# A second receiver for turned attention tiles in batch 3 of a convolution and attention kernel

## The chip, the cores and the metric

The kernel runs on one core of a Trainium2 chip. The metric is the device time of one execution in microseconds (us), the median of three runs. An execution is one launch of the whole program on one set of inputs; all data is float32.

## The reference, cut to what matters

The input is four images (batches) of 128 channels by 64 x 64 positions. Layer 0 normalises by groups, takes a deformable 3 x 3 convolution (bilinear samples at computed places, then a matrix product) and adds it to the input. Layer 1 treats each image as 4096 tokens of 128 channels. What the change touches is its attention:

```
qkv    = _qz_ring(heads + rx_theta)                 # 16 heads of 8 numbers a token
scores = einsum('bhsd,bhtd->bhst', q, q) / sqrt(8)  # q is both query and key
attn   = softmax(scores, axis=-1)
ctx    = einsum('bhst,bhtd->bhsd', attn, q)         # and value
t      = t + _ln(x1 + ffn_out, ...)                 # projection, feed-forward, norms
t      = t + experts(_ln_t(t))                      # top 2 of 8 experts
```

Since q is query and key, the scores are symmetric: the exponentials of the scores between the tokens s and t serve for the queries s and, transposed, for the queries t. There is no causal mask, so each batch has 16 heads x 4096 x 4096 exponentials if no use is made of this.

## The kernel before, in words

**Tiling.** The 4096 tokens of a batch are 8 chunks of 512, and the 16 heads are 4 groups of 4. A *run* is the attention of one group for the 512 queries of one chunk (batch b, group g, chunk sc). A *step* of a run takes 128 keys (t from 0 to 31, four to a chunk): `scores` (L1261) makes four matmuls into two PSUM tiles `sc`, ScalarE makes two exponentials `e<-sc` of 128 x 1024 (L1270), and `context` (L1281) multiplies the exponentials with values and a column of ones into `acc`, which holds both the weighted sum and the denominator. There are three `sc` tiles and six `e` tiles. At the end of a run VectorE copies `acc` to `cu` (L1493) and it is parked in DRAM.

**Giving and taking.** `gifts(b, g, sc)` (L1295) names the chunks to which a run gives: before, the next one. For each given key tile, `turn` (L1135 to L1156) transposes the two `e` tiles in blocks of 32 on VectorE (L1140) into a tile `st` (three buffers, `NST`), and SyncE (SP) stores it to a DRAM slot `etd` (L1149, 1 MB). `add_run` leaves the taken key tiles out of the taker's list `ts` and spreads the given ones evenly over the giver's. The taker fetches each tile with one transfer on SP's queue (`fetch`, L1189, the transfer at L1195, 1 MB) into a buffer `et` (`NET` = 2 buffers), and `from_turned` (L1201) multiplies it into `acc` in two halves of 8 matmuls (L1214): it replaces four score matmuls, two exponentials and four context matmuls of a step. `granted` and `returned` count the `et` buffers; a fetch that finds none waits in `asking`, and is issued when a tile has been multiplied.

**Order of the runs.** Batch 3 goes chunk by chunk, and in a chunk over its four groups (`LOTS[3]`). Its chunk 0 takes nothing and has 32 steps a run; chunks 1 to 7 take 4 tiles from the chunk before and have 28 steps a run. That is 912 steps in batch 3, of 3700 in all.

**The order on the engines is fixed when the program is built.** The main loop (from L1417) emits the steps for PE, VectorE, GpSimd and SP by hand; each engine executes its list in order. Between two steps the planner `Beside` (L65) adds pieces of side work: the next batch's preparation, the turned halves (job "turned", rank -1, so ahead of all else), and *finishes* (`finish`, L1084: projection, feed-forward and experts of one chunk, with about forty short groups of matmuls, each with VectorE work behind it). It keeps a model clock that advances by 1.82 a step, lets one piece with matmuls in per step, gains 0.44 of PE time a step at most (`RATE`), and puts a piece off while VectorE's planned work is too far behind. Up to two finishes are open at a time; a chunk is finished after its fourth group. What is still open after the last step is emitted by `beside.drain()`, one job after the other. At the end of each run `drain("turned")` emits what is left of the taken tiles.

**Other transfers.** Before each run its keys and values (`kT` 256 KB and `qf` 72 KB a chunk, L1239 and L1241) are loaded chunk by chunk, also on SP's queue, leaving out the chunks that are taken. The buffer `xs` (18 KB a partition, one buffer) holds the gathered samples for the convolution; its last use is batch 3's preparation, which is over before batch 3's runs begin.

Of the kernel before, what the change touches and what calls it, by code (L numbers as in the profile page):

```python
# [9 lines left out]
F32 = mybir.dt.float32  # L10
# [12 lines left out]
P = 128  # L23
# [5 lines left out]
CH = 512  # L29
NCH = NPOS // CH  # L30
KK = 9
# [17 lines left out]
NET = 2  # L49
# [153 lines left out]
def need(pe=0.0, dve=0.0, lat=0.0, hold=False, after=0.0):  # L203

    return pe, dve, lat, hold, after
# [17 lines left out]
def kernel(  # L225
# [23 lines left out]
    NB = x.shape[0]  # L249
# [4 lines left out]
    big = ctx.enter_context(tc.tile_pool(name="big", bufs=1))  # L254
    work = ctx.enter_context(tc.tile_pool(name="work", bufs=2))
# [5 lines left out]
    beside = Beside()  # L261
# [156 lines left out]
    for i in range(NFX):  # L418
        t = big.tile([P, 4, QR], F32, name=f"fx{i}")
        nc.gpsimd.memset(t, 0.0)  # L420
        h = t[:, :, : HEADS * QW].rearrange("p j (h d) -> p j h d", d=QW)
# [735 lines left out]
    def etd_slot(g, sc, t):  # L1157
        key = g, t // 4 % 3, t // 4 - sc, t % 4
        if key not in etd:
            etd[key] = dram.tile([P, 4, 4 * P], F32, name="etd" + "_".join(map(str, key)))  # L1160
        return etd[key]

    room = [NET]
    asking = []

    def granted(emit):
        if room[0]:
            room[0] -= 1
            emit()
        else:  # L1170
            asking.append(emit)

    def returned():
        if asking:
            asking.pop(0)()
        else:
            room[0] += 1

    def fetch_values(run):
        b, g, _ = runs[run][:3]  # L1180
# [5 lines left out]
            )  # L1186
            values[run, giver] = q

    def fetch(run, giver, kt):  # L1189
        _, g, sc = runs[run][:3]  # L1190
        t = 4 * sc + kt
        if (g, giver, t) in turning:
            beside.flush()
        e = work.tile([P, 4, 4, P], F32, tag="et", name=f"et{run}_{giver}_{kt}", bufs=NET)
        nc.sync.dma_start(  # L1195
            out=e.rearrange("p r h x -> p r (h x)"),
            in_=etd_slot(g, giver, t).rearrange("(r i) o x -> i o r x", i=32),
        )
        fetched[run, giver, kt] = e, beside.now + 16.0

    def from_turned(run, acc):  # L1201

        for giver in takes[run]:
            qv = values.pop((run, giver)).rearrange("p t x -> p (t x)")
            for kt in range(4):
                while (run, giver, kt) not in fetched:
                    yield need(lat=1.0)
                e, landed = fetched.pop((run, giver, kt))
                for half in range(2):
                    yield need(pe=MM256, hold=None, after=landed)  # L1210
                    for t in (2 * half, 2 * half + 1):
                        for h in range(4):
                            at = QG * t + QW * h
                            nc.tensor.matmul(  # L1214
                                acc[32 * h : 32 * h + QW, P * kt : P * (kt + 1)],
                                lhsT=qv[:, at : at + QW],
                                rhs=e[:, :, h, 32 * t : 32 * (t + 1)],
                                start=False, stop=False,
                            )
                returned()  # L1220

    keys, queries, values = {}, {}, {}
    turning, storing = set(), set()
# [2 lines left out]
    fetched = {}  # L1226
# [67 lines left out]

    def gifts(b, g, sc):  # L1295
        first = (4 if g == NGRP - 1 else 3) if b == 0 else 0
        return [sc + 1] if first <= sc < NCH - 1 else []


    def add_run(b, g, sc, chunks, kind):  # L1300
# [55 lines left out]
    for n, (run, t) in enumerate(steps):  # L1356
        b, g, sc = runs[run][:3]
# [32 lines left out]
    def at_hand(step, n):  # L1390

        run, t = steps[step]
        b, g, sc = runs[run][:3]
        wanted = [(b, g, t // 4)]

        def missing():
            return any(l[0] in wanted and l[3] <= step for l in loads)

        if missing():
            load_next(n, wanted)  # L1400
        load_queries(run)
        if missing() or run not in queries:
            return False
        early = b == 0 and run < opening + 40
        return not early or max([landing[run]] + [landing[k] for k in wanted]) <= beside.now

    es = []
    n = issued = begun = 0
    beside.rate = 1.0
    with tc.manual_schedule(engines={PE, DVE, SP, POOL}):  # L1410
        alone.append(True)
        beside.add("prepare", prepare(0), 2)
        while (0, 0) not in prepared:
            beside.force("prepare")
        beside.flush()
        alone.clear()
        while n < len(steps):  # L1417
            if issued < len(steps) and issued <= n + LAG and at_hand(issued, n):
                es.append(scores(*steps[issued]))
                issued += 1  # L1420
            elif issued <= n:
                if beside.has("prepare"):
                    beside.force("prepare")
                else:
                    beside.now += beside.STEP
                    beside.flush(beside.now)
                continue
            run, t = steps[n]
            b, g, sc, ts, kind = runs[run]
            following = runs[run + 1] if run + 1 < len(runs) else None  # L1430
            at = n - ends[run]
            streaming = run < opening
            for m in (n, n + 1):
                if m < issued and steps[m] in gives:
                    gives.remove(steps[m])
                    turn(es[m - n], *steps[m])

            beside.fills = 3 if run < 12 else 1
            if streaming:
                backlog = 1.5  # L1440
            else:
                backlog = 0.4 if at >= len(ts) - 3 else 3.2
            if b + 1 < NB:

                share = (n - begun) / (of_batch[b] - 80 - begun)
                beside.rank("prepare", 2 if progress.get(b + 1, 0.0) > share else 0.5)
            beside.step(backlog)
            if issued <= n + LAG and issued < len(steps) and at_hand(issued, n):
                continue
            load_next(n)  # L1450
            if t == ts[0]:
                if kind in (MORE, LAST):
                    if (g, sc) in storing:
                        beside.flush()
                    cu = work.tile([P, 512], F32, tag="cu", name=f"cu{run}", bufs=NCU)
                    nc.sync.dma_start(out=cu, in_=partd[g][sc])
                if run == opening:
                    beside.rate = beside.RATE
                acc = ps_a.tile([P, 512], F32, tag="acc", name=f"acc{run}")
                if not beside.has("prepare") and b + 1 < NB and (b + 1, 0) not in prepared:  # L1460
                    beside.rate = beside.RATE
                    begun = n
                    beside.add("prepare", prepare(b + 1), 2)
            if at == len(ts) - 1:
                beside.drain("turned")
            if following:
                if following[0] != b and at == 0:
                    beside.drain("prepare")

                if at == 1:  # L1470
                    load_queries(run + 1)
                    if len(ts) <= 8 and run + 2 < len(runs):
                        load_queries(run + 2)
                if takes[run + 1] and at == len(ts) - 5:
                    fetch_values(run + 1)
                    for giver in takes[run + 1]:
                        for kt in range(4):
                            granted(lambda a=(run + 1, giver, kt): fetch(*a))
            by_act = run < opening
            context(acc, run, t, es.pop(0), cu if by_act and kind == MORE else None)  # L1480
            n += 1
            if at == 0 and takes[run]:
                beside.add("turned", from_turned(run, acc), -1)
            if at < len(ts) - 1:
                continue
            if not by_act:
                beside.dve = max(beside.dve, beside.now + 1.9) + ve(512)
            if kind in (WHOLE, FIRST):
                cu = work.tile([P, 512], F32, tag="cu", name=f"cu{run}", bufs=NCU)
            if by_act:  # L1490
                nc.scalar.copy(cu, acc)  # L1491
            elif kind in (WHOLE, FIRST):
                nc.vector.tensor_copy(cu, acc)  # L1493
            else:
                nc.vector.tensor_tensor(cu, cu, acc, ALU.add)
            if kind in (WHOLE, LAST):
                park_context(b, g, sc, cu)
            else:
                park_sums(g, sc, cu, beside.now + 3.0 if by_act else beside.dve)
        alone.append(True)  # L1500
        beside.drain()
# [73 lines left out]
```

## Time and profile before

| what | value |
|---|---|
| runs | 7573.33, 7592.69, 7599.12 us; median 7592.69 |
| profiled execution | 7579.71 us; its span from first to last instruction 7576.5 us |
| mean granted TensorE clock | 0.968 |
| busy, share of the span | PE 94%, ScalarE (ACT) 91%, VectorE (DVE) 59%, GpSimd (POOL) 22% |
| exponentials `e<-sc` | 7400 of 1081 ns (they overlap: 6849.4 us in all) |
| turned tiles | 396 stored, 396 fetched, 1 MB each |
| all DMA | 1689.51 MB, mean 223 GB/s |
| last exponential ends | 7491.9 us after the start |

The page of a profile gives the busy time of each engine, the span in 40 slices, the chain of work that ended last and the costliest groups of instructions. A view by stretches gives the busy time of each engine between two times, the granted clock, and the share and rate of the 16 DMA engines; a timeline lists the instructions of an engine by start and duration. Matmul ends are modelled, so the distance between starts says more of PE than its busy share. Batch 3's runs lie between about 5805 and 7492 us.

### The profile page before, as it was taken

How to read it: one execution, taken by the hardware profiler on the slowest of the kernel's cores; microseconds unless marked ns; L12 is line 12 of the kernel's file. 1: busy time of each engine (PE TensorE's matmuls, PEld its weight loads, DVE VectorE, ACT ScalarE, POOL GpSimd, SP SyncE). 2: the span in 40 equal slices, each digit the busy share in tenths (PEclk: the TensorE clock that was granted, in tenths of full speed). 3: DMA queues.
4: the chain of work that ended last, by engine and by line, in shares of the span. 5: the costliest groups of instructions: out<-in, count | busy, mean ns of one | idle time of the engine just before them, and what ended most of it. 6: DMA issues, size and time to landing. Idle time of an engine off the chain costs nothing.

```text
span 7576.5 us, 180754 instructions
## 1 busy us (share of the span) xinstructions
PE 7113.9 (94%) x73848; PEld 2375.9 (31%) x73848; DVE 4465.9 (59%) x8950; ACT 6863.5 (91%) x7467; POOL 1653.2 (22%) x1326
## 2 busy tenths in 40 slices
PE   3688999899999999999999999999999999999997
PEld 2122222223333333333333323333333333333333
DVE  7755356667444877776544677775444554455434
ACT  0578999889999999999999998989999999999995
POOL 5544034443000433422000334431000000000000
PEclk6889999999999999999999999999999999999998
DMA  6777567978446878887655789897454466666661
GB/s 181 223 204 219 141 223 241 300 234 291 149 168 200 292 244 280 268 277 244 203 179 190 228 279 298 289 324 237 174 190 152 148 236 230 232 222 239 226 202 63
DMA packets 909788, 1689.51 MB, mean 223 GB/s; under 512 B 150754, under 2 KB 384124, under 8 KB 858268
## 3 DMA queue, kind: packets, MB, share of 16 engines
q1 hardware_dynamic: 809102, 1371.37, 54.9%
q0 software_dynamic: 92160, 302.06, 12.4%
q8 instruction: 579, 9.49, 0.5%
q10 hardware_dynamic: 7694, 4.52, 0.2%
q14 instruction: 253, 2.07, 0.1%
HBM read 1027.51 MB, written 650.14 MB: 221 GB/s over the span
## 4 chain that ended last, share of the span: by engine, by line
PE 80%; DMA 8%; DVE 4%; issue 2%; ACT 2%; SPq 1%; another core or an unknown queue 0%; POOL 0%; POOLq 0%; DVEq 0%; ACTq 0%
PE acc L1281 39%; PE sc L1261 24%; PE acc L1214 5%; PE e_ps L281 4%; PE conv_ps L281 3%; DMA et<-etd 2%; PE f_ps L281 2%; ACT e L1270 2%; DMA etd<-st 1%; DMA sT<-smd 1%; PE om_ps L533 1%; DMA smd<-tr 1%; DVE st L1140 1%; DVE v L645 1%; DMA cu<-part 1%
## 5 line engine op out<-in xcount | busy, mean ns | idle before, releaser
L1270 ACT ACTIVATE e<-sc 128x1024 f32<-128x1024 f32 x7400 | 6849.4, 1081 | 527.0 <-PE sc L1261 368.1
L1281 PE MATMUL acc<-e,qf 128*9 128x512 f32 (+1 forms) x29600 | 3938.3, 601 | 18.6 <-ACT cu L1491 7.5
L1261 PE MATMUL sc<-qT,kT 32*128 32x512 f32 x14800 | 2368.7, 499 | 153.3 <-ACT e L1270 84.8
L1261 PEld LDWEIGHTS sc<-qT,kT 32*128 32x128 f32 x14800 | 942.8, 183 | 3612.6 <-ACT e L1270 3130.4
L625 POOL DMA_INDIRECT v<-tab,idx x1152 | 1451.8, 1260 | 1579.3 <-DVE tr L686 956.2
L1140 DVE STREAM_TRANSPOSE st<-e 128x1024 f32<-128x1024 f32 x792 | 937.3, 1222 | 752.4 <-ACT e L1270 620.1
L1281 PEld LDWEIGHTS acc<-e,qf 128*9 128x9 f32 (+1 forms) x29600 | 682.4, 91 | 610.3 <-issue 346.8
L396 POOL TENSOR_TENSOR r<-ln_t,expo 128x4 f32<-128x4 f32 x96 | 112.2, 1169 | 3105.4 <-DVE ln_t L394 3057.0
L645 DVE TENSOR_TENSOR v<-v,wt 128x1536 f32<-128x1536 f32 x384 | 667.0, 1737 | 119.5 <-DMA v<-tab,idx 96.8
L1214 PE MATMUL acc<-et,qv 128*9 128x128 f32 x12672 | 506.4, 276 | 52.2 <-DMA et<-etd 44.6
L1065 DVE TENSOR_TENSOR eo<-e_ps,gt 128x512 f32<-128x512 f32 x256 | 175.2, 686 | 552.5 <-PE e_ps L281 547.5
L650 DVE TENSOR_TENSOR v<-v 128x768 f32<-128x768 f32 x384 | 367.2, 956 | 10.1
L281 PE MATMUL conv_ps<-sT,wconv_sb 128*32 128x256 f32 x4320 | 351.0, 399 | 15.7 <-DMA sT<-smd 11.6
L1214 PEld LDWEIGHTS acc<-et,qv 128*9 128x9 f32 x12672 | 270.0, 90 | 254.4 <-issue 212.6
L686 DVE STREAM_TRANSPOSE tr<-v 128x128 f32<-128x128 f32 x1080 | 249.4, 282 | 37.5 <-DMA etd<-st 28.7
L1493 DVE COPY cu<-acc 128x512 f32<-128x512 f32 x116 | 80.2, 692 | 306.3 <-PE acc L1281 260.8
L651 DVE TENSOR_TENSOR v<-v 128x384 f32<-128x384 f32 x384 | 215.7, 562 | 13.3
L396 POOL TENSOR_TENSOR rstd<-lt_t,expo 128x4 f32<-128x4 f32 x32 | 57.9, 1811 | 575.9 <-DVE lt_t L394 550.7
L281 PE MATMUL f_ps<-w_sb,h 128*32 128x128 f32 x4096 | 166.1, 282 | 0.1
L950 DVE TENSOR_SCALAR h<-h_ps,b_sb 128x512 f32<-128x512 f32 x128 | 94.9, 744 | 100.3 <-PE h_ps L948 89.9
L823 POOL COPY fx<-rn 128x512 f32<-128x512 f32 x32 | 26.8, 838 | 526.3 <-DVE rn L822 321.4
L965 DVE TENSOR_TENSOR a<-a,f_ps 128x512 f32<-128x512 f32 x32 | 21.9, 685 | 198.8 <-PE f_ps L281 198.8
(227 smaller groups left out, 3166.9 us busy)
## 6 DMA issues: line engine op xcount, KB each, us to landing
etd<-st SPq DMA_DIRECT2D x396, 1024.0 KB
et<-etd SPq DMA_DIRECT2D x396, 1024.0 KB
kT<-kTd SPq DMA_DIRECT2D x372, 256.0 KB
smd<-tr SPq DMA_DIRECT2D x360, 192.0 KB
sT<-smd SPq DMA_DIRECT2D x360, 192.0 KB
qT<-qTd SPq DMA_DIRECT2D x166, 256.0 KB
atd<-cu SPq DMA_DIRECT2D x128, 256.0 KB
qf<-fqd SPq DMA_DIRECT2D x372, 72.0 KB
```

Of the source, the lines that this page charges most:

```text
L281: nc.tensor.matmul(dst[c : c + 32], lhsT=lhsT[:, c : c + 32], rhs=rhs, start=start, stop=stop)
L625: nc.gpsimd.indirect_dma_start(out=v[:, k, :], out_offset=None, in_=tab, in_offset=bass.IndirectOffsetOnAxis(ap=idx[:, j, kk : kk + 1], ax ...
L645: nc.vector.tensor_tensor(v4, v4, w12[:, :, None].to_broadcast([P, 12, C]), ALU.mult)
L650: nc.vector.tensor_tensor(v[:, :, : 2 * C], v[:, :, : 2 * C], v[:, :, 2 * C :], ALU.add)
L651: nc.vector.tensor_tensor(v[:, :, :C], v[:, :, :C], v[:, :, C : 2 * C], ALU.add)
L686: nc.vector.transpose(out=tr9[:, k, :, j % 4, :], in_=v[:, k, :C].rearrange("p (c i) -> p c i", i=32),)
L1065: nc.vector.tensor_tensor(ws[hf], pe.rearrange("p (e c) -> p e c", c=C), gt[:, i, 4 * hf : 4 * (hf + 1), None].to_broadcast([P, 4, C]), AL ...
L1140: nc.vector.transpose(out=st[:, :, 2 * pr : 2 * pr + 2, :].rearrange("p o h (q j) -> p o (h q) j", j=32), in_=es[pr].rearrange("p h (q o i ...
L1214: nc.tensor.matmul(acc[32 * h : 32 * h + QW, P * kt : P * (kt + 1)], lhsT=qv[:, at : at + QW], rhs=e[:, :, h, 32 * t : 32 * (t + 1)], star ...
L1261: nc.tensor.matmul(ps[i // 2][:, i % 2, :], lhsT=kT[h : h + 32, P * (t % 4) : P * (t % 4 + 1)], rhs=qT[h : h + 32, :], start=True, stop=True,)
L1270: nc.scalar.activation(e, ps[pr], AF.Exp, scale=1.0 / math.sqrt(HD))
L1281: nc.tensor.matmul(acc[32 * h : 32 * h + width, :], lhsT=flat[:, first : first + width], rhs=es[h // 2][:, h % 2, :], start=(t == ts[0]), ...
```

## The change

In batch 3, chunks 0, 2 and 4 give to the next chunk and to the one after. So chunks 2, 4 and 6 take 8 tiles a run (24 steps, before 28), and chunks 0, 2 and 4 turn 8 (before 4). Two views into the `xs` buffer, each of the size of one turned tile, are added as places for received tiles six steps before the end of batch 2's last run; `room` becomes a list of places, and a fetch into one of them is planned to land after 10 instead of 16 of the model clock. Nothing else differs.

```diff
-    room = [NET]
+    room = [None] * NET
     asking = []
 
     def granted(emit):
-        if room[0]:
-            room[0] -= 1
-            emit()
+        if room:
+            emit(room.pop(0))
         else:
             asking.append(emit)
 
-    def returned():
+    def returned(place):
         if asking:
-            asking.pop(0)()
+            asking.pop(0)(place)
         else:
-            room[0] += 1
+            room.append(place)
...
-    def fetch(run, giver, kt):
+    def fetch(run, giver, kt, place):
...
-        e = work.tile([P, 4, 4, P], F32, tag="et", name=f"et{run}_{giver}_{kt}", bufs=NET)
+        e = place
+        if e is None:
+            e = work.tile([P, 4, 4, P], F32, tag="et", name=f"et{run}_{giver}_{kt}", bufs=NET)
...
-        fetched[run, giver, kt] = e, beside.now + 16.0
+        fetched[run, giver, kt] = e, place, beside.now + (16.0 if place is None else 10.0)
...
     def gifts(b, g, sc):
         first = (4 if g == NGRP - 1 else 3) if b == 0 else 0
-        return [sc + 1] if first <= sc < NCH - 1 else []
+        if not first <= sc < NCH - 1:
+            return []
+        return [sc + 1, sc + 2] if b == NB - 1 and sc in (0, 2, 4) else [sc + 1]
...
+                if following[0] == NB - 1 != b and at == len(ts) - 6:
+                    spare_et = big.tile([P, KK, CH], F32, tag="xs", name="spare_et")
+                    spare_et = spare_et.rearrange("p k n -> p (k n)")
+                    for i in range(2):
+                        place = spare_et[:, 4 * CH * i : 4 * CH * (i + 1)]
+                        room.append(place.rearrange("p (r h x) -> p r h x", r=4, h=4))
```

More of the change, by code (lines that the diff above doesn't have):

```diff
@@ L1207, in from_turned @@
                     yield need(lat=1.0)
-                e, landed = fetched.pop((run, giver, kt))
+                e, place, landed = fetched.pop((run, giver, kt))
                 for half in range(2):
@@ L1219, in from_turned @@
                             )
-                returned()
+                returned(place)
     keys, queries, values = {}, {}, {}
@@ L1477 @@
                         for kt in range(4):
-                            granted(lambda a=(run + 1, giver, kt): fetch(*a))
+                            granted(lambda place, a=(run + 1, giver, kt): fetch(*a, place))
             by_act = run < opening
```

## The prediction

> **What bounds the kernel now.** I read the page first, then batch 3 by stretches of one chunk, then the timelines of PE and of the end. The stretches give per chunk: length, busy time (and count) of PE, PEld, DVE, ACT, POOL, then granted clock, DMA share and GB/s. Here are chunks 0, 2, 4, 6 and 7.
>
> ```profile
> 5805.00:6041.00 236.00, 235.91 (x2309) 75.69 (x2305) 135.46 (x320) 235.98 (x259) 7.05 (x7) 1.00 0.44 144
> ...
> 6249.00:6456.00 207.00, 206.62 (x2340) 71.40 (x2338) 104.02 (x228) 206.52 (x227) 4.03 (x4) 1.00 0.67 231
> ...
> 6663.00:6870.00 207.00, 206.26 (x2346) 71.56 (x2342) 103.41 (x215) 206.74 (x228) 3.02 (x3) 1.00 0.65 223
> ...
> 7077.00:7284.00 207.00, 207.00 (x2335) 71.21 (x2327) 95.75 (x189) 206.94 (x227) 3.02 (x3) 1.00 0.67 229
> 7284.00:7492.00 208.00, 207.69 (x2378) 73.07 (x2382) 60.78 (x189) 207.74 (x228) 5.34 (x5) 1.00 0.41 132
> ```
>
> ScalarE never idles, DVE is half free, and the DMA engines stand at two thirds. PE's column is full too, so one step has to be looked at (start, duration, group, on PE):
>
> ```profile
> 6522.38 0.51 PE L1261 MATMUL sc<-qT,kT 32*128 32x512 f32 x4
> 6522.82 0.62 PE L1214 MATMUL acc<-et,qv 128*9 128x128 f32 x16
> 6523.26 1.04 PE L1281 MATMUL acc<-e,qf 128*9 128x512 f32 x8
> 6524.23 0.51 PE L1261 MATMUL sc<-qT,kT 32*128 32x512 f32 x4
> ```
>
> From start to start, scores take 0.44, a turned half 0.44, the context 0.97: 1.85 us a step, and 1.41 without the half. On ACT, 36 exponentials took 33.32 us, 0.925 each, so 1.85 a step as well. Steps without a half last about as long (scores at 6516.53, 6518.28, 6520.11), so ScalarE sets the pace of batch 3 and PE just keeps up. 912 steps by 1.85 make 1687 us, the length of the stretches.
>
> The second thing that counts is the end. The last exponential ends at 7491.9 and the span at 7576.5, so 84.6 us hold no attention at all, only finishes: half of the experts of chunk 6, then all of chunk 7. On VectorE (start, duration, group):
>
> ```profile
> 7503.93 0.69 DVE L892 COPY y_6T<-y_ps 128x512 f32<-128x512 f32 x1 [0.57 <-PE y_ps L890]
> 7504.54 0.54 DVE L1097 RECIPROCAL rd<-rd 128x64 f32<-128x64 f32 x1
> 7505.00 0.63 DVE L899 TENSOR_TENSOR r<-r,vec_sb 128x512 f32<-128x512 f32 x1
> 7510.16 0.69 DVE L901 TENSOR_TENSOR aT<-aT,a 128x512 f32<-128x512 f32 x1 [4.54 <-DMA a<-rdd]
> ...
> 7545.56 0.69 DVE L892 COPY u_7T<-u_ps 128x512 f32<-128x512 f32 x1 [0.57 <-PE u_ps L890]
> ...
> 7572.14 0.69 DVE L892 COPY y_7T<-y_ps 128x512 f32<-128x512 f32 x1 [0.57 <-PE y_ps L890]
> ```
>
> A finish that stands alone takes 68.2 us (7503.93 to 7572.14), its part from the copy of u on 26.6 (7545.56 to 7572.14). It is a chain of short dependent instructions: DVE is busy for 41.7 us of it.
>
> **The change part by part.**
>
> *Steps that go.* Three chunks x 4 groups x 4 tiles = 48 steps, 96 exponentials. At 1.85 that is **-88.8 us**, all on the bounding engine, if nothing else is late.
>
> *Turned halves on PE.* 48 x 0.88 = 42 us come, 48 x 1.41 = 68 us go, and a step with a half still fits 1.85: nothing.
>
> *Turning on DVE.* 96 transposes of 1.22 us, 117 us in chunks 0, 2 and 4. In a run of chunk 2 that is 8 x 2.44 = 19.5 us of 44.4, beside a DVE that was busy for half: nothing by itself. But each reads two of the six e tiles and writes one of three st tiles, so if a store is late, the turn waits, then the e tiles, then ScalarE.
>
> *Transfers.* 48 stores and 48 fetches of 1.05 MB come, 101 MB; some key loads go. A run of chunk 2 or 4 now moves 16 x 1.05 = 16.8 MB of tiles, 6 x 0.336 of keys and values, about 1.0 of the rest: 19.8 MB. The same count for a run before gives 11.3 in 51.8 us, 219 GB/s, beside rows of 223 to 231. In 24 x 1.85 = 44.4 us 19.8 MB need 446 GB/s. The trace shows no such rate. In stretches of 6 us where the DMA share is about 1 or over, I find 294 to 409 GB/s, mean 359 over 50 of 220 stretches of batch 3. Two of them:
>
> ```profile
> 6634.00:6640.00 6.00, 6.00 (x92) 2.30 (x84) 5.39 (x12) 6.00 (x8) 0.00 (x0) 1.00 1.07 377
> 7046.00:7052.00 6.00, 6.00 (x66) 1.94 (x58) 4.18 (x8) 6.00 (x8) 0.00 (x0) 1.00 1.04 409
> ```
>
> At 360 a run takes 55.0 us, 10.6 over its steps: 42 a chunk. Some of that can be put off into the next, lighter chunk: three stores (3.1 MB, 9 us) and about 5 us of the lead of the first four fetches. So 28 a chunk, 56 for chunks 2 and 4. Chunk 6 takes 8 and gives 4: 15.6 MB, 43.3 us at 360 against 44.4, close enough for some late tiles: 4. **+60 us**. The bounds: at 409 a run takes 48.4, 16 a chunk less the same 14, so some 5 in all; at 342 (0.67 share for 229 GB/s) it takes 57.9, 80 in all with chunk 6's 5 on top, and gaps in the queue bring it to 100. The four places are no escape: a place comes free only when its tile is multiplied, and SP issues in order.
>
> The Trainium skill speaks for less than this. Its page "DMA: Bandwidth & Descriptors", section Measured, has 425 GB/s for transfers of 16 MB on a core whose neighbour idles. By that estimate a run would take 46.6 us, the overhang would disappear in the slack, and the sum below would be near 7645. No stretch here reaches it, and the mean is 359, so the rows stand.
>
> *The finishes.* This is the largest term, and the diff does not show it. Turned halves go ahead of finishes, one piece with matmuls fits in a step, and the turns fill VectorE's planned time. In batch 3 the steps without a half fall from 912 - 224 = 688 to 864 - 320 = 544, and in the 24-step runs nearly nothing is left. I counted in the instruction order of both built programs how many of the 32 finishes are wholly emitted by the end of each chunk of batch 3:
>
> | end of chunk | 0 | 1 | 2 | 3 | 4 | 5 | 6 | 7 |
> |---|---|---|---|---|---|---|---|---|
> | before | 19 | 21 | 23 | 24 | 26 | 27 | 29 | 30 |
> | after | 19 | 21 | 21 | 23 | 24 | 25 | 26 | 28 |
>
> After the last scores there remain, in this order on PE and on DVE: of chunk 4 all from the transposes of u on; chunk 6 whole; chunk 7 whole; chunk 5 from the projection on (its reciprocal is done earlier). The engines execute in order and the jobs stand one behind the other, as chunk 6 and 7 do now. So: 2.4 us from the last exponential to the copy of u (three contexts, the transposes, as at 7490.18 to 7492.98 and 1.26 of u), 26.6, 68.2, 68.2, then 68.2 less the 4.5 of waiting for `a` and 0.5 of the reciprocal = 63.2, and 4.4 to the end as now (7572.14 to 7576.5): 233 us in place of 84.6, **+148**. Bounds: part of chunk 4 runs while the granted clock is still high (1.00 until 7500, 0.50 at 7504), some 8 less; late loads of the next finish, some 7 more: 140 to 155.
>
> *The places and the allocation.* Two views of xs and one wait on the last convolution of batch 3's preparation, drained before: nothing; were that cover gone, one landing of a fetch, a few us.
>
> **Sum:** -88.8 + 60 + 148 = +119. On the profiled execution's 7579.7 that is 7699; on the median of the runs, 13 us higher, 7712. I take 7705. The last exponential would end near 7463, and 233 us follow.
>
> **Rivals.**
> - *The transfers keep up* (5 in place of 60): 7580 or 7593 - 88.8 + 5 + 148, about 7650. For it: stretches at 408, and stores that may be put off. Against it: 446 wanted.
> - *The transfers cost more* (100): 7740 or, with the upper tail, 7755. For it: in the built program's order nearly every transfer on SP waits for the one eight before it, and SP waits in order for PE to free a place and for DVE to turn; each such wait leaves the DMA engines short. Against it: when SP is late, what it waits for has already happened.
> - *Faster: the finishes at the end overlap.* If the waits of one were filled by another, the end would cost DVE's busy time: 3 x 41.7 + 18 for the rest of chunk 4 + 7 = 150, so +65; without stalls the sum is -24, 7556 to 7569. The point of decision is an end of 173 us (84.6 + 88.8) with no stall. Against it: DVE's list has all of one finish before the next.
> - *That it does not do what it says* is excluded: the built program has 7304 exponentials for 7400, and 444 fetches and stores for 396.
>
> **Chances.** Forecast (stalls 25 to 85) 0.62; transfers keep up 0.18; cost more 0.15; overlap 0.03; something between, near no change, 0.02. Within 0.3% (23 us, about what a measurement can tell from no change): 0.02; faster 0.03; slower 0.95. Range: low 7580 - 88.8 + 5 + 140 = 7636; high 7593 - 88.8 + 100 + 155 = 7759: 7635 to 7760.
>
> **What would show it.** Right: some 864 steps in batch 3, the last exponential near 7463; stretches of chunks 2 and 4 about 205 us long with a DMA share over 0.9 and idle ACT, chunk 6 about 180, odd chunks 207 as before; from the last exponential to the end about 233 us, with three copies of y after 63 to 68 us each. Wrong: chunks 2 and 4 of 178 us with a busy ACT (transfers keep up); ACT idle in odd chunks (stalls spread further); an end well under 200 us (finishes overlap), or DVE turns that wait though the DMA share is low.

## The result and the profile after

The changed kernel takes 7685.07 us (7669.29 to 7689.69, four runs) against 7593.91 us of the kernel before, run beside it: a ratio of 1.0126, 95% interval 1.0111 to 1.0142. It is slower. The profiled execution took 7689.69 us, its span 7687.9.

The view by stretches of the changed kernel, in chunks 2, 4, 6 and 7 of batch 3 and from the last exponential to the end (columns as in the prediction):

```profile
6266.00:6457.00 191.00, 184.56 (x2362) 71.00 (x2358) 113.68 (x207) 178.73 (x195) 4.89 (x5) 1.00 1.03 395
...
6664.00:6864.00 200.00, 186.38 (x2428) 71.55 (x2424) 104.12 (x136) 179.35 (x193) 1.01 (x1) 0.97 1.02 386
...
7071.00:7248.00 177.00, 176.83 (x2464) 68.30 (x2460) 69.16 (x124) 177.00 (x192) 3.02 (x3) 1.00 0.96 351
7248.00:7452.00 204.00, 203.81 (x2356) 71.40 (x2356) 71.16 (x210) 203.56 (x223) 5.04 (x5) 1.00 0.41 134
7452.00:7688.00 236.00, 96.99 (x1138) 56.48 (x1132) 142.09 (x421) 0.92 (x4) 9.07 (x9) 0.62 0.06 17
```

In the ACT column, chunks 2 and 4 lost 12 and 21 us of their length with the DMA share over 1, chunk 6 lost nothing. The last row is the price: 236 us in which ScalarE has 0.92 us of work. VectorE's copies in it name the four finishes (timeline of the end, start, duration, group):

```profile
7453.42 0.68 DVE L892 COPY u_4T<-u_ps 128x512 f32<-128x512 f32 x1
...
7479.92 0.69 DVE L892 COPY y_4T<-y_ps 128x512 f32<-128x512 f32 x1 [0.57 <-PE y_ps L890]
...
7548.06 0.69 DVE L892 COPY y_6T<-y_ps 128x512 f32<-128x512 f32 x1 [0.57 <-PE y_ps L890]
...
7615.84 0.69 DVE L892 COPY y_7T<-y_ps 128x512 f32<-128x512 f32 x1 [0.57 <-PE y_ps L890]
...
7683.96 0.69 DVE L892 COPY y_5T<-y_ps 128x512 f32<-128x512 f32 x1 [0.57 <-PE y_ps L890]
```

The distances are 26.5, 68.1, 67.8 and 68.1 us: the rest of chunk 4, then three finishes one after the other, each as long as the one that stood alone before.

A chunk is counted here, and in the experiments, from the copy `cu` that ends the run before it to the copy that ends its own last run.

| stretch, us | before | after | difference |
|---|---|---|---|
| start to batch 3's first step | 5813.0 | 5823.5 | +10.5 |
| batch 3 to its last exponential | 1678.9 | 1628.2 | -50.7 |
| of it chunk 2 / 4 / 6 | 207.1 / 207.6 / 206.3 | 191.2 / 200.6 / 177.3 | -15.9 / -7.0 / -29.0 |
| last exponential to the end of the span | 84.6 | 236.2 | +151.6 |

The first row is not the change: up to one key load at the end of batch 2, the built orders are the same there, and executions of one kernel differ by 26 us (7573 to 7599).

### The profile page after: what moved, and what is told of

It is laid out like the page before. It is cut to its first block, busy times and chain, and to the rows that moved or that the text cites. A ratio compares the mean times of both kernels' runs of the same rounds, so it can differ in the third digit from the quotient of the medians.

```text
span 7687.9 us, 182740 instructions
## 1 busy us (share of the span) xinstructions
PE 7112.2 (93%) x74808; PEld 2411.3 (31%) x74808; DVE 4574.0 (59%) x9046; ACT 6782.1 (88%) x7371; POOL 1665.3 (22%) x1326
## 4 chain that ended last, share of the span: by engine, by line
PE 79%; DMA 10%; DVE 4%; issue 2%; ACT 2%; SPq 1%; another core or an unknown queue 0%; POOL 0%; ACTq 0%; POOLq 0%; DVEq 0%
PE acc L1282 38%; PE sc L1262 23%; PE acc L1215 6%; PE conv_ps L281 4%; PE e_ps L281 3%; ACT e L1271 2%; PE f_ps L281 2%; DMA et<-etd 2%; DMA etd<-st 2%; DMA sT<-smd 1%; PE om_ps L533 1%; DMA kT<-kTd 1%; DVE st L1140 1%; DMA cu<-part 1%; PE ao_ps L281 0%
## 5 line engine op out<-in xcount | busy, mean ns | idle before, releaser
L1271 ACT ACTIVATE e<-sc 128x1024 f32<-128x1024 f32 x7304 | 6767.1, 1076 | 562.6 <-PE sc L1262 371.0
L1282 PE MATMUL acc<-e,qf 128*9 128x512 f32 (+1 forms) x29216 | 3882.6, 601 | 17.1 <-DVE cu L1502 7.6
L1262 PE MATMUL sc<-qT,kT 32*128 32x512 f32 x14608 | 2339.4, 500 | 183.0 <-ACT e L1271 112.3
L1140 DVE STREAM_TRANSPOSE st<-e 128x1024 f32<-128x1024 f32 x888 | 1051.0, 1222 | 910.9 <-ACT e L1271 722.1
L1215 PE MATMUL acc<-et,qv 128*9 128x128 f32 x11648 | 470.5, 277 | 57.4 <-DMA et<-etd 47.2
L1215 PEld LDWEIGHTS acc<-et,qv 128*9 128x9 f32 x11648 | 248.9, 90 | 246.8 <-issue 203.0
L1502 DVE COPY cu<-acc 128x512 f32<-128x512 f32 x116 | 80.2, 692 | 314.7 <-PE acc L1282 268.8
```

Source lines behind the costliest of these rows:

```text
L1140: nc.vector.transpose(out=st[:, :, 2 * pr : 2 * pr + 2, :].rearrange("p o h (q j) -> p o (h q) j", j=32), in_=es[pr].rearrange("p h (q o i ...
L1215: nc.tensor.matmul(acc[32 * h : 32 * h + QW, P * kt : P * (kt + 1)], lhsT=qv[:, at : at + QW], rhs=e[:, :, h, 32 * t : 32 * (t + 1)], star ...
L1262: nc.tensor.matmul(ps[i // 2][:, i % 2, :], lhsT=kT[h : h + 32, P * (t % 4) : P * (t % 4 + 1)], rhs=qT[h : h + 32, :], start=True, stop=True,)
L1271: nc.scalar.activation(e, ps[pr], AF.Exp, scale=1.0 / math.sqrt(HD))
L1282: nc.tensor.matmul(acc[32 * h : 32 * h + width, :], lhsT=flat[:, first : first + width], rhs=es[h // 2][:, h % 2, :], start=(t == ts[0]), ...
```

## Experiments

The first four kernels ran together, then the fifth to eighth, the ninth and the tenth, each set with its own runs of the kernel before. The chips of the fifth to ninth reach batch 3 some 100 to 130 us sooner, whatever the kernel; where nothing stalls, the lengths of batch 3's chunks agree across chips within 1 us, so these and the ratios are compared, not the totals.

**e1: the places alone.**

```diff
-        return [sc + 1, sc + 2] if b == NB - 1 and sc in (0, 2, 4) else [sc + 1]
+        return [sc + 1]
```

> Two more places, but every chunk gives to the next one alone, as before. My theory (the loss is finishes that are left to the end, and transfers in chunks 2 and 4): no change, 7593 within 20, last exponential 40 us before 7532 give or take, i.e. batch 3 of 912 steps at 1.85, an end of 80 to 85 us. Rival (the places do harm by themselves, because four fetches of 1 MB now start together and keys come late): 7610 or more, with idle ScalarE in the chunks 1 to 7.

Measured 7583.02 against 7582.73: ratio 1.0008 (0.9994 to 1.0021). Chunks 1 to 7 take 207 us but one, chunk 4 with 212.4 and a single wait of ScalarE of 5.7 (VectorE waited 7.4 us there for `a`, a small load of a finish); the end is 80.2. The places cost nothing that can be measured in the total.

**e2: the gifts alone** (the block that makes the two places is left out).

> The new gifts without the two places: 8 tiles go through 2 buffers in a run of 24 steps. My theory: the fetches are now a chain (fetch, multiply, fetch), the planner runs out of steps and emits the rest at the run's end, PE waits there, so all 12 runs of chunks 2, 4 and 6 are longer than 50 us, chunk 6 too though it has fewer transfers; an end of about 235 us; 7780 in all (7720 to 7850). Rival (the rate of the DMA engines alone decides, the number of places does not): as the changed kernel, 7685 within 15, chunk 6 at 177.

Measured 7820.09: ratio 1.0315 (1.0290 to 1.0340). Chunks 2, 4 and 6 take 243.4, 239.6 and 236.3 us, the end 230. Chunk 6 decides: by stretches

```profile
7158.00:7394.00 236.00, 204.70 (x2505) 77.81 (x2505) 76.19 (x159) 177.50 (x194) 3.02 (x3) 0.91 0.75 262
```

its DMA engines are at 0.75 and ScalarE still works only 177.5 of 236 us. The waits there (who waited for whom: us, times, longest):

```profile
DVE cu L1496 <- PE acc L1282: 65.2, 4, 17.6
...
PEld acc L1215 <- DMA et<-etd: 34.8, 11, 5.4
PE acc L1215 <- DMA et<-etd: 30.2, 11, 5.1
```

PE waits for tiles that are fetched one pair at a time. So the places are needed: with them chunk 6 takes 177.3.

**e3: the finishes of the end in turn.**

```diff
         alone.append(True)
+        while beside.has("finish"):
+            beside.force("finish")
         beside.drain()
```

> The changed kernel, but the finishes left at the end are emitted piece by piece in turn from two jobs, the one that can begin earliest by the model clock first, and not job by job. The attention part is the same instruction by instruction. My theory (the end of 236 us is the loss): the waits of one finish are filled by the other, the end shrinks to about 150 us (130 to 175) and the time to 7600 (7580 to 7620). Rival (the loss is in the attention part, from transfers): 7670 to 7690.

Measured 7626.79: ratio 1.0066 (1.0042 to 1.0091), half of the loss. Batch 3 to its last exponential is 1627.4 us, as with the change. The end, by stretches:

```profile
7437.00:7625.00 188.00, 94.88 (x1140) 55.32 (x1136) 139.11 (x421) 0.93 (x5) 9.07 (x9) 0.68 0.07 21
```

188 for 236, with the same work (139 us of VectorE for 142). The mechanism was as I expected, the size not: I had an end of 150, near VectorE's busy time, and 7580 to 7620 in all. With two jobs in turn, 49 us of waits are left beside VectorE's work.

**e4: two pieces of side work a step in batch 3.**

```diff
-            beside.fills = 3 if run < 12 else 1
+            beside.fills = 3 if run < 12 else 2 if b == NB - 1 else 1
```

> The changed kernel with two pieces of side work a step in batch 3 (one before) and no limit by the credit: by the order of the built program 31 of 32 finishes are emitted by the end of chunk 7, and only chunk 7's is left. My theory: the end shrinks to about 75 us, PE has room for it in sum (864 x 1.41 + 160 x 0.88 + about 200 = 1560 against 1598 us of ScalarE), the last exponential ends at 7450 to 7475, and the time is 7545 (7525 to 7570), faster than the kernel before. Rival 1 (steps with two pieces last 2.29 on PE, and what the end wins is lost there): last exponential at 7490 or later, 7570 to 7600. Rival 2 (the loss lies in the transfers): about 7670.

Measured 7632.74: ratio 1.0076 (1.0052 to 1.0101). The end is 78 us, as expected, but the last exponential comes at 7549.5: batch 3 takes 1742.5 us to it, 114 more than with the change. The mechanism of the first rival was right, though its 7570 to 7600 was too low as well. PE's timeline in chunk 1 (start, duration, group):

```profile
6099.56 0.51 PE L1262 MATMUL sc<-qT,kT 32*128 32x512 f32 x4
6099.99 1.07 PE L281 MATMUL e_ps<-ew_sb,u_4T 128*32 128x256 f32 x16
6100.88 1.04 PE L1282 MATMUL acc<-e,qf 128*9 128x512 f32 x8
6101.85 0.50 PE L1262 MATMUL sc<-qT,kT 32*128 32x512 f32 x4
```

A step with two pieces lasts 2.29 us, 0.44 more than ScalarE needs. Over batch 3 ScalarE waited for scores (who waited for whom: us, times, longest):

```profile
ACT e L1271 <- PE sc L1262: 109.0, 237, 7.7
```

In sum that is nearly the 114; with the change these waits are 2.1 us in all. Six of the 237 are long, 31 us in sum, most of them beside a late load of a finish (the longest beside VectorE's wait of 7.7 us for `rd`). The other 231, 78 us in sum, have a median of 0.35: that is the price of second pieces. The free 0.44 of other steps does not pay it back. I put that down to the three `sc` tiles, which hold only half a step of lead; no run has more of them. My sum over the whole batch (1560 against 1598) was an average, and the average hid this.

**e5: the added transfers out to DRAM left out.** The second gifts are transposed, not stored, and the fetch reads the tile stored for the next chunk: part of the attention is computed from other keys.

```diff
+        if t // 4 - sc == 2:
+            return
         slot = etd_slot(g, sc, t)
...
-            in_=etd_slot(g, giver, t).rearrange("(r i) o x -> i o r x", i=32),
+            in_=etd_slot(g, giver, t - 4 if sc - giver == 2 else t).rearrange("(r i) o x -> i o r x", i=32),
```

> Leaves out the 48 added stores: the tiles for the chunk after the next are transposed but not stored, and the fetch reads the tile that was stored for the next chunk, so the output is not the reference's. ScalarE, PE and VectorE do the same work; a run of chunks 2 and 4 moves 15.6 in place of 19.8 MB. My theory (the 14 and 23 us that chunks 2 and 4 lie over 177 come from the DMA engines): both take 177 to 180, chunk 6 177, the end as in the changed kernel (about 240), 7645 to 7660 in all. Rival (they come from the added transposes, or from PE waiting on the chain of places): chunks 2 and 4 stay at 190 to 200.

One run, 7523.21 beside 7461.93 of the kernel before on that chip. Chunks 2 and 4 by stretches:

```profile
6134.00:6312.00 178.00, 177.46 (x2374) 67.61 (x2367) 113.55 (x207) 177.62 (x196) 5.03 (x5) 1.00 0.97 351
6518.00:6696.00 178.00, 177.67 (x2438) 67.30 (x2438) 104.28 (x137) 177.93 (x194) 1.01 (x1) 1.00 0.99 357
```

ScalarE is busy throughout, with the same VectorE time as with the change (113.55 beside 113.68, 104.28 beside 104.12). So the stalls came from the transfers, not from turning or from PE. Without the stores the `st` tiles also come free at once; the run does not separate this from the bytes. The end is 237.8, about as with the change.

**e6: the kernel before with the mixed end**, a control (the diff of e3).

> The kernel before with the mixed end of the third experiment: a control. Its end holds half of the experts of chunk 6 and chunk 7. My theory: those two overlap by 12 us at most, 7575 to 7590, the same within what can be measured. Rival (mixing is a gain of its own, for any end): 40 us faster, 7545.

Ratio 1.0004 (0.9995 to 1.0013), end 81.5, for 84.6. Mixing gains little where less than two finishes are left.

**e7: turned halves take no finish's place.**

```diff
-                    yield need(pe=MM256, hold=None, after=landed)
+                    yield need(pe=MM256 if runs[run][0] < NB - 1 else 0.0, hold=None, after=landed)
```

> The changed kernel, but in batch 3 the planner counts a turned half as work without matmuls, so it takes no finish's place in a step; the halves that have landed are emitted at once, beside a finish piece. By the built order 31 finishes are emitted by the end of chunk 7 (28 in the changed kernel); with VectorE's planned time for the turns set to nothing instead it is 29. My theory: the end is 75 us again, but steps with two pieces last longer than ScalarE's 1.85, as in the fourth experiment, so the last exponential moves from 7452 to 7520 or later: 7590 to 7640. Rival (PE has room for all of it, and the fourth experiment lost its time to something else): last exponential near 7455, 7530.

Measured 7538.10 against 7461.93: ratio 1.0116 (1.0099 to 1.0132), where my upper bound was 0.6% over the kernel before. The end is 78.9, so it is the places of the halves that kept the finishes out; but batch 3 to its last exponential takes 1760 us for 1628. This is not the loss of e4 over again. A piece that counts as work without matmuls is not held to one a step, and PE runs the halves in eights, 3.5 us at a stretch (chunk 1; x16 is one half):

```profile
5934.28 0.93 PE L1262 MATMUL sc<-qT,kT 32*128 32x512 f32 x4
5935.14 0.64 PE L281 MATMUL e_ps<-ew_sb,u_3T 128*32 128x256 f32 x8
5935.60 1.93 PE L1215 MATMUL acc<-et,qv 128*9 128x128 f32 x64
5937.35 1.93 PE L1215 MATMUL acc<-spare_et,qv 128*9 128x128 f32 x64
5939.09 1.04 PE L1282 MATMUL acc<-e,qf 128*9 128x512 f32 x8
```

All 320 halves of batch 3 stand in 40 such eights. ScalarE's waits for scores are few and long:

```profile
ACT e L1271 <- PE sc L1262: 151.8, 44, 14.6
```

Of the 44, 32 last 2.7 to 3.5 us, about the length of an eight; the longest stands beside VectorE's wait of 12.6 us for `a`, a load of a finish. So this run shows what bunched halves cost. What the finishes would cost with halves and pieces spread evenly, it does not show.

**e8: one giving chunk, two pieces a step in chunk 7 only, mixed end.**

```diff
-        return [sc + 1, sc + 2] if b == NB - 1 and sc in (0, 2, 4) else [sc + 1]
+        return [sc + 1, sc + 2] if b == NB - 1 and sc in (0,) else [sc + 1]
...
+            beside.fills = 3 if run < 12 else 2 if b == NB - 1 and sc == 7 else 1
```

> Only chunk 0 gives to two chunks (16 tiles, 12 transfers a run in chunk 2 alone), two pieces of side work a step in chunk 7 only, and the mixed end. By the built order 30 finishes are out by the end of chunk 7, as before the change. My theory: -29.6 of steps, no stall, +10 to 20 in chunk 7, an end of 78 to 85: 7570 (7555 to 7585), just faster than before. Rival (a step with two pieces costs as much as the finish it saves): 7590 to 7600.

Measured 7466.09 against 7461.93: ratio 1.0002 (0.9992 to 1.0011). Chunk 2 takes 178.1, a gain of 29 with 0.92 DMA share; the end is 82. Chunk 7 gives 24 of it back (228.9 for 204.9) and chunk 3 gives 9, where VectorE stood 9.2 us before a reciprocal whose small load was late. The rival was right: 1.0002 is 7595 beside the 7593.91 of the first set.

**e9: two giving chunks that do not meet** (the diff of e8 with `sc in (0, 3)`).

> Chunks 0 and 3 give to two chunks (32 tiles; no run takes 8 and gives 8, so 12 transfers a run at most), two pieces a step in chunk 7 only, and the mixed end. By the built order 30 finishes are out by the end of chunk 7, and of chunk 6 26 of 36 pieces of matmuls remain. My theory: -59 of steps, no stall, +10 to 20 in chunk 7, an end of about 105 (20 more than before): 7570 (7550 to 7590). Rival (runs with 12 transfers of 1 MB stall on the DMA engines, at 344 GB/s on average): chunks 2, 3 and 5 are 5 us or more a run over their steps, 7600 or more.

Measured 7455.00 against 7460.50: ratio 0.9989 (0.9980 to 0.9998), the only version that is faster than the kernel before, by a tenth of a per cent, with an interval that just leaves out no change. Chunk 2 gains 29 and chunk 5 20; chunk 7 gives back 23, the end 15, chunk 3 7. In chunk 7, the one with two pieces a step, ScalarE waits 17.4 us for scores in 53 waits, none over 0.6. The rival's stalls did not come: the eight 24-step runs, with 12 transfers each, kept 44 to 45 us at 325 to 352 GB/s, except one of 52.8; in chunk 3 one run took 58.7.

**e10: e9 with a later reciprocal** (`lat=9.0` for `lat=4.0` between a finish's loads and its reciprocal, batches 2 and 3).

> The ninth kernel, with 9 in place of 4 of the model clock between the loads of a finish and its reciprocal (batch 2 and 3). In the ninth, single runs of chunks 3 and 5 were 7 to 8 us over their steps, and there VectorE waited up to 8 us for small loads of a finish that stood behind turned tiles. My theory: those waits block the turns behind them and go with the longer lead; 8 to 15 us less in chunks 3 and 5, 2 to 5 us more at the end (75 rows of PE remain, 71 before): ratio to the kernel before 0.997 to 0.999. Rival (the runs are long for another reason, such as bunched finish pieces): chunks 3 and 5 as in the ninth, 0.999 to 1.001.

Measured 7594.89 against 7586.16: ratio 1.0010 (1.0001 to 1.0018). Chunk 3 lost its stall (205.6 for 213.6), as I thought, but chunk 5 kept a run of 55, chunk 4 is 3.5 longer, chunk 7 is 4 longer and the end is 111: 29 finishes are done by the end of chunk 7, for 30 in e9. In the total the rival was right. What holds that one run of chunk 5 (VectorE before `a`, loaded last in a finish, 8.2 us in e9) was not settled.

## Why the prediction was right

It said 7705 and slower, the runs 7685: +112 by the prediction, +91 by the medians. By its terms, against the profiled execution, the change is -88.8 + 37 + 152 = +100; the other 10.5 of that pair of executions lie before batch 3.

- *Steps that go, -88.8.* Right: 96 exponentials fewer, and where nothing stalls (chunk 6, e5) a run of 24 steps takes 44.4.
- *Transfers, +60.* The mechanism was right (e5), the size too large: chunks 2 and 4 lie 14 and 23 over 177.6, chunk 6 not at all, 37 in sum. In chunk 2 the path that I named is there: VectorE's turns waited 47.3 us for stores, and ScalarE for turns. These are ScalarE's exponentials in chunk 2 and in chunk 4 (behind the second bar the idle time before them and what ended it), and the turns' waits in chunk 2:

```profile
L1271 ACT ACTIVATE e<-sc 128x1024 f32<-128x1024 f32 x194 | 180.8, 1072 | 12.3 <-PE acc L1282 6.2 <-DVE st L1140 5.0 <-PE u_ps L890 0.3
...
L1271 ACT ACTIVATE e<-sc 128x1024 f32<-128x1024 f32 x196 | 183.3, 1057 | 20.6 <-DVE st L1140 17.1 <-PE sc L1262 2.1 <-PE y_ps L890 0.2
...
DVE st L1140 <- DMA etd<-st: 47.3, 16, 6.4
```

  The mis-sized term is the rate. I took 360 GB/s, the mean of short stretches at full share; under a long flow of turned tiles the rows show 395 and 386, and single runs up to 405. Why the short stretches were slower was not measured. At 395 and 386 a run takes 50.1 and 51.3 us, and the same sum gives 9 and 14 a chunk, 23 in place of 56. The rate alone would thus give too little: 5 us more in chunk 2 are not accounted for (6.2 us of ScalarE's waits there ended with a context, which I had not foreseen), and 9 more in chunk 4 lie in one run, which took 56.3. The Trainium skill ("DMA: Bandwidth & Descriptors", Measured) has 425 GB/s, which is above what these rows show; the sum that goes with it, no stall, fails too.

  The run of 56.3 shows another path. Between 6800 and 6870 the waits have

```profile
DVE rd L1097 <- DMA rd<-atd: 13.8, 1, 13.8
DVE st L1140 <- DMA etd<-st: 13.6, 4, 3.8
...
ACT e L1271 <- DVE st L1140: 9.1, 1, 9.1
```

  so a small load of a finish, issued on SP's queue at 6813.1 behind four fetches and used at 6825.6, held VectorE's list, the turn behind it, and ScalarE. I had named the store buffers, not the finishes' own loads.
- *The finishes, +148.* Measured 151.6. The order of the built program gave the jobs, and the trace of before their lengths. e3, e4 and e7 show three times that this term is real: when the finishes overlap or leave the end, the end is shorter. Within it one part was off: chunk 5 took 68.1, not 63.2, for it too waited 4.9 us for `a`; the few us at both ends were shorter than I had.
- *PE, +0.* Right for the kernel as changed (chunk 6 keeps 1.85 a step), but thinner than I wrote. e4 puts the displaced finishes back as second pieces of a step, and 114 us come back in batch 3 for the 158 that the end lost. So the loss is not only a matter of order at the end: what the turned halves took are places in PE's steps, and a second piece in a step makes ScalarE wait (78 of the 114 us; about 31 more belong to late loads). e7 does not tell this, since its 132 us come from halves in eights. Whether smaller pieces, spread evenly, would fit into PE's free time was not tried.
- *Places, 0.* Right for their cost (e1). What they are for is shown by e2: without them 2% more is lost.

The rival of overlapping finishes was excluded by the in-order list, and e3, which makes them overlap, still leaves a loss.

Two figures of the working were slightly off and decide nothing: the finish that stood alone keeps VectorE busy for 41.1 us by the view of that stretch, not 41.7; and with 1.0 of the rest a run before counts 11.7 MB, or 227 GB/s, not 11.3 and 219.

## What to carry to other kernels

When two engines stand close to level, work taken from one and given in smaller measure to the other moves the limit: price what the second engine's free time was used for, here the side work that then runs alone at the end. Look at what the planner emits after the main loop, in the built order, before believing a sum over the loop. Averages over a batch do not tell whether a step fits: in e4 and in chunk 7 of e9, steps with two pieces made ScalarE wait some 0.3 us at a time, which the next ones did not give back. And a piece that the planner counts as free may be emitted in a bunch, as the halves of e7.

## What the runs showed of the hardware that I had not expected

- In chunks 2 and 4 of the changed kernel the DMA engines moved 378 to 405 GB/s over runs of 44 to 51 us at a share of 1.01 to 1.03, more than the mean of the saturated 6 us stretches of before (359).
- Small loads of a finish, issued on SP's queue among the 1 MB transfers, kept VectorE waiting for 13.8 us in the changed kernel, 12.6 in e7, 9.2 in e8 and 7.4 in e1, and each time ScalarE stood still for 5.7 us or more in the same run.
- Chips differ by up to 1.8% in the same program (7460.50 to 7593.91 for the kernel before), nearly all of it before batch 3: the difference grows through batches 0 to 2, while each chunk of batch 3 takes the same time within 1 us (the traces of before and of e6). What differs in the chips was not found.
